# Attention softmax: where the division by the row sums is done, and which buffers the position products use

## The chip, the cores and the metric

The kernel runs on one core of one Trainium2 chip. A core has five engines with their own instruction streams: TensorE (PE in the profile, its weight loads are PEld), VectorE (DVE), ScalarE (ACT), GpSimd (POOL) and SyncE (SP), which here only issues transfers. Sixteen DMA engines move data between the memory on chip (SBUF) and DRAM. TensorE writes into a small accumulator memory (PSUM). The metric is the device time of one execution in microseconds (us); the median of three runs is given.

## The reference, cut to what matters

Two layers of attention over images, each with a group normalization ahead of it and a residual behind it. There are 4 images of 32 by 32 positions, so 1024 positions with 768 channels each, and 12 heads of 64 channels. All is in 32-bit floats. The second layer differs in the weights' layout, in biases on q, k and v, and in one more scale factor on q.

```python
qkv = x @ Wqkv                                   # x is normalized by groups first
q, k, v = ...                                    # (4 * 12, 1024, 64) each
rel_h = einsum('bhwc,hkc->bhwk', r_q, Rh)        # position terms: q times a table of
rel_w = einsum('bhwc,wkc->bhwk', r_q, Rw)        #   relative rows and columns
bias = rel_h[..., :, None] + rel_w[..., None, :]
scores = scale * einsum('bqc,bkc->bqk', q, k) + bias.reshape(B * hn, S, S)
attn = softmax(scores, axis=-1)                  # exp(scores - max) / sum
out = einsum('bqk,bkc->bqc', attn, v)            # the value product
return out @ Wproj + bproj                       # + residual outside
```

The division by the softmax's sum is a factor for each query row. It can be done on the 1024 probabilities of a row ahead of the value product, or on the 64 results of the row behind it.

## The kernel before

The work is cut into 8 images (2 layers of 4), in each 6 pairs of heads (called g, 48 in all), and in each pair 8 blocks of 128 queries (called n). A unit is one block of one pair: two heads, 128 queries, 1024 keys. Only TensorE's order is fixed by hand; on the other engines and on the transfer queue a scheduler at build time chooses the order. The three parts below are those that the change touches. SP issues nearly all transfers, in its own order, and an issue that has to wait holds those behind it.

```python
scpool = ctx.enter_context(tc.tile_pool(name="sc", bufs=6))   # 128 x 1024 score tiles
tbpool = ctx.enter_context(tc.tile_pool(name="tb", bufs=4))   # transposed, two blocks each
ptpool = ctx.enter_context(tc.tile_pool(name="pt", bufs=1))   # probabilities, keys on partitions
ps_s   = ctx.enter_context(tc.tile_pool(name="ps_s", bufs=3, space=PSUM))
ps_m   = ctx.enter_context(tc.tile_pool(name="ps_m", bufs=2, space=PSUM))

def project_in(g, which, i):          # q, k, v of pair g, half i: six matmuls "pj"
    if i == 0:
        pool, tag = (scpool, "sc") if which == 2 else (qkpool, "qk"[which])
        qkv_of[g, which] = pool.tile([P, S], FP, tag=tag, ...)    # v takes a score buffer
    ...                               # q leaves PSUM on ACT (L236, L238), k and v on DVE
    if which == 0:
        early.append(lambda: positions(g, i))
    ...

def positions(g, i):                  # position products "tp" (L276)
    ps = ps_s.tile([P, 2, 4, P], FP, tag="s", ...)
    ...                               # 8 small matmuls of q with the table
    t = scpool.tile([P, 4, 2, P], FP, tag="sc", name=f"t_{g}_{i}")   # a score buffer too
    nc.scalar.copy(t, ps.rearrange("p h j r -> p j h r"))         # L281
    nc.scalar.dma_start(out=td[i * HALF : (i + 1) * HALF, :]..., in_=t...)   # tdr<-t
    if i == 1:
        ...                           # 16 small reads from DRAM: rel<-tdr (L298), on SP

def biases(g, n):
    for h in range(2):
        sc = scpool.tile([P, HW, HW], FP, tag="sc", ...)
        nc.gpsimd.tensor_tensor(sc, <rel rows>, <rel columns>, ALU.add)      # L308

def scores(g, n):
    ps = [ps_s.tile([P, S], FP, tag="s", ...) for h in range(2)]
    ...                               # four matmuls "s" (L320)
    st = small.tile([P, 3, 2], FP, tag="sm", ...)
    for h in range(2):
        nc.vector.tensor_tensor_reduce(out=sc, in0=ps[h], in1=sc, ...,
                                       accum_out=st[:, 0, h : h + 1])        # L327: add, row max
        nc.scalar.activation(sc, sc, AF.Exp, bias=..., accum_out=st[:, 1, h : h + 1])   # L331
    nc.vector.reciprocal(st[:, 2, :], st[:, 1, :])                           # L335
    for h in range(2):
        nc.gpsimd.tensor_scalar(sc, sc, st[:, 2, h : h + 1], 1.0, ALU.mult, ALU.mult)   # L338

def turn(g, n):                       # keys onto partitions, by way of DRAM
    for h in range(2):
        nc.vector.transpose(tb[:, :, j, :], sc_of[g, n, h])                  # L356
        if j == 1:                    # every second block
            nc.sync.dma_start(out=td, in_=tb...)                             # L359: td<-tb
            nc.sync.dma_start(out=pt[:, quarter]..., in_=td...)              # L360: pt<-td

def weigh(g, half):                   # value products "av" of four blocks (L372)
    ...                               # 16 matmuls of 128 x 512, two heads side by side
    for q in range(2):
        nc.vector.tensor_copy(attn_of[g]..., av...)                          # L379
```

The main loop, cut. `todo` holds the projections of the next pair (36 matmuls) and parts of the output projection (12 matmuls "o", whose sums leave PSUM at L432 and L434); a block takes six of them.

```python
for at, (g, n) in enumerate(units):
    ...
    run(early)                        # position products and issues that have become possible
    scores(next unit)
    biases(unit after it)
    turn(g, n)
    take(todo, -(-left(todo) // (NT - n)))
    if n % 4 == 1 and at > 4:
        weigh(*(units[at - 2][0], n // 4 ^ 1))     # the half that ended two blocks ago
    run(ready)                        # v turned on TensorE, "vt" (L261)
```

Of the kernel before, what the change touches and what calls it, by code (L numbers as in the profile page):

```python
# [31 lines left out]
P = 128  # L32
# [16 lines left out]
def attention_blocks(ctx: ExitStack, tc: tile.TileContext, a: dict, out: bass.AP):  # L49
# [8 lines left out]
    qkpool = ctx.enter_context(tc.tile_pool(name="qk", bufs=2))  # L58
    vpool = ctx.enter_context(tc.tile_pool(name="v", bufs=2))
    scpool = ctx.enter_context(tc.tile_pool(name="sc", bufs=6))  # L60
    tbpool = ctx.enter_context(tc.tile_pool(name="tb", bufs=4))
    ptpool = ctx.enter_context(tc.tile_pool(name="pt", bufs=1))
    relpool = ctx.enter_context(tc.tile_pool(name="rel", bufs=2))
    iopool = ctx.enter_context(tc.tile_pool(name="io", bufs=4))
# [146 lines left out]
    def project_in(g, which, i):  # L211

        im, pair = divmod(g, NP)
        l = images[im][0]
        xn, w = xn_of[im], w_of[g, which]
        cols = slice(i * HALF, (i + 1) * HALF)
        if i == 0:
            pool, tag = (scpool, "sc") if which == 2 else (qkpool, "qk"[which])
            qkv_of[g, which] = pool.tile([P, S], FP, tag=tag, name=f"{'qkv'[which]}_{g}")
        to = qkv_of[g, which][:, cols]  # L220
        if which == 2:
            to = qkv_of[g, 2].rearrange("p (k j y) -> p y k j", y=4, k=NT)[:, 2 * i : 2 * i + 2]
        t = ps_m.tile([P, HALF], FP, tag="m", name=f"pj_{g}_{which}_{i}")
        for c in range(NC):
            nc.tensor.matmul(  # L225
                t, lhsT=w[:, c, :], rhs=xn[c][:, cols],
                start=(c == 0), stop=(c == NC - 1),
            )
            if c < NC - 1:
                yield True  # L230
        if which == 2:
            t = t.rearrange("p (y k j) -> p y k j", y=2, k=NT)
        bias = bqkv[:, which, pair : pair + 1]
        if which == 0:
            if l == 0:
                nc.scalar.activation(to, t, AF.Copy, scale=SCALE)  # L236
            else:
                nc.scalar.activation(to, t, AF.Identity, bias=bias, scale=SCALE * SCALE)  # L238
        elif l == 0:
            nc.vector.tensor_copy(to, t)  # L240
        else:
            nc.vector.tensor_scalar(to, t, bias, None, ALU.add)
        if which == 0:
            early.append(lambda: positions(g, i))
        if which == 2 and i == 1:
            late.extend([lambda: turn_values(g, 0), lambda: turn_values(g, 1)])
        if i == 1 and g + 1 < NPAIR:
            early.append(lambda: load_w(g + 1, which))
        if which == 2 and i == 1 and pair == NP - 1 and im + 1 < NI:
            early.extend([lambda: load_x(im + 1), lambda: norm_stats(im + 1)])  # L250
        yield True
# [12 lines left out]
    def positions(g, i):  # L264

        l = images[g // NP][0]
        q = qkv_of[g, 0]
        if i == 0:
            t_of[g] = dram2.tile([S, 2 * P], FP, tag="tdr", name=f"tdr_{g}")
            rel_of[g] = relpool.tile([P, 2, 2, NT, HW], FP, tag="rel", name=f"rel_{g}")  # L270
        ps = ps_s.tile([P, 2, 4, P], FP, tag="s", name=f"tp_{g}_{i}")
        for j in range(4):
            for h in range(2):
                rows = slice(h * D, (h + 1) * D)
                at = 4 * i + j
                nc.tensor.matmul(  # L276
                    ps[:, h, j, :], lhsT=q[rows, at * P : (at + 1) * P], rhs=tabs[l][rows, :],
                    start=True, stop=True,
                )
        t = scpool.tile([P, 4, 2, P], FP, tag="sc", name=f"t_{g}_{i}")  # L280
        nc.scalar.copy(t, ps.rearrange("p h j r -> p j h r"))  # L281
        td = t_of[g]
        nc.scalar.dma_start(
            out=td[i * HALF : (i + 1) * HALF, :].rearrange("(j p) r -> p j r", p=P),
            in_=t.rearrange("p j h r -> p j (h r)"),
        )
        if i == 1:
            for h in range(2):
                for ax in range(2):
                    for y in range(4):  # L290


                        at = HW * y * 2 * P + h * P + HW - 1 + 2 * HW * ax - (y if ax == 0 else 0)
                        src = bass.AP(
                            td.tensor, td.offset + at,
                            [[2 * P - ax, HW], [P * 2 * P - (4 if ax == 0 else 0), NT], [1, HW]],
                        )
                        nc.sync.dma_start(out=rel_of[g][32 * y : 32 * y + 32, h, ax, :, :], in_=src)  # L298


    sc_of, tb_of, pt_of, attn_of = {}, {}, {}, {}

    def biases(g, n):
        rel = rel_of[g]
# [8 lines left out]
    def scores(g, n):  # L313
        q, k = qkv_of[g, 0], qkv_of[g, 1]
        ps = [ps_s.tile([P, S], FP, tag="s", name=f"s_{g}_{n}_{h}") for h in range(2)]
        for i in range(2):
            cols = slice(i * HALF, (i + 1) * HALF)
            for h in range(2):
                rows = slice(h * D, (h + 1) * D)
                nc.tensor.matmul(  # L320
                    ps[h][:, cols], lhsT=q[rows, n * P : (n + 1) * P], rhs=k[rows, cols],
                    start=True, stop=True,
                )
        st = small.tile([P, 3, 2], FP, tag="sm", name=f"sm_{g}_{n}")
        for h in range(2):
            sc = sc_of[g, n, h].rearrange("p y x -> p (y x)")
            nc.vector.tensor_tensor_reduce(  # L327
                out=sc, in0=ps[h], in1=sc, scale=-1.0, scalar=BIG, op0=ALU.add, op1=ALU.min,
                accum_out=st[:, 0, h : h + 1],
            )  # L330
            nc.scalar.activation(  # L331
                sc, sc, AF.Exp, bias=st[:, 0, h : h + 1], scale=-1.0,
                accum_out=st[:, 1, h : h + 1],
            )
        nc.vector.reciprocal(st[:, 2, :], st[:, 1, :])  # L335
        for h in range(2):
            sc = sc_of[g, n, h].rearrange("p y x -> p (y x)")
            nc.gpsimd.tensor_scalar(sc, sc, st[:, 2, h : h + 1], 1.0, ALU.mult, ALU.mult)  # L338

    def turn(g, n):  # L340

# [23 lines left out]
    def weigh(g, half):  # L365
        if half == 0:
            attn_of[g] = apool.tile([P, S], FP, tag="attn", name=f"attn_{g}")
        av = ps_m.tile([P, HALF], FP, tag="m", name=f"av_{g}_{half}")
        for k in range(NT):
            for h in range(2):  # L370
                rows = slice(h * D, (h + 1) * D)
                nc.tensor.matmul(  # L372
                    av[rows, :], lhsT=v_of[g][:, k, rows],
                    rhs=pt_of[g, half, h][:, :, :, k, :].rearrange("p q r t -> p (q r) t"),
                    start=(k == 0), stop=(k == NT - 1),
                )
        for q in range(2):
            at = half * HALF + q * 2 * P
            nc.vector.tensor_copy(  # L379
                attn_of[g][:, at : at + 2 * P].rearrange("p (n r i) -> p r n i", n=2, r=4),  # L380
                av[:, q * 2 * P : (q + 1) * 2 * P].rearrange("p (r n i) -> p r n i", n=2, r=4),
            )


# [54 lines left out]

    early, late = [], []

    def run(todo):
        while todo:
            todo.pop(0)()
# [30 lines left out]
    with tc.manual_schedule(engines={mybir.EngineType.PE}):  # L477
# [13 lines left out]
        for at, (g, n) in enumerate(units):  # L491
            im, pair = divmod(g, NP)
            end = im + 1 == NI
            if n == 0:
                ins = prepare(g + 1) if g + 1 < NPAIR else []
                if pair < 3:
                    todo = ins + (put_out(im - 1, 1, range(4 * pair, 4 * pair + 4)) if im else [])
                elif pair < NP - 1:
                    todo = ins + ([] if end else put_out(im, 0, range(4 * pair - 12, 4 * pair - 8)))
                elif not end:  # L500
                    outs = put_out(im, 0, range(8, 12))
                    stages = [(staged(f), 0) for f in norm_apply(im + 1)]
                    todo = [x for both in zip(outs, stages) for x in both] + ins
            if end and pair == NP - 1 and n == 2:
                todo = put_out(im, 0, range(12))
            run(early)
            if at + 1 < len(units):
                scores(*units[at + 1])
            if at + 2 < len(units):
                biases(*units[at + 2])  # L510
            ready = late[:1]
            del late[:1]
            turn(g, n)
            take(todo, -(-left(todo) // (NT - n)))
            if n % 4 == 1 and at > 4:
                weigh(*(units[at - 2][0], n // 4 ^ 1))
            run(ready)
# [53 lines left out]
```

## Time and profile before

The three runs took 4016.77, 4021.23 and 4022.7 us; the median is 4021.23 us. One execution was profiled; its span is 4008.2 us.

| engine | busy, share of the span | largest group of instructions |
| --- | --- | --- |
| TensorE | 95% | L225, projections of q, k and v, 3456 records |
| VectorE | 58% | L356 transposes and L327 add with row maximum, 768 each |
| GpSimd | 57% | L308 position biases, 768 |
| ScalarE | 29% | L331 exponentials, 768 |
| 16 DMA engines | between 70% and 80% in most of the run | td<-tb and pt<-td, 384 transfers of 1 MB each |

A busy share is time in which at least one instruction of an engine runs. A matmul on 32-bit floats shows as two records. The profile's page also lists groups of instructions with what they waited for, the transfers with the time from issue to landing, and the waits by pairs of waiter and releaser; in a timeline the number in brackets is the idle time of the engine ahead of an instruction and what ended it. Names are those of the program's tiles: `sc` a score tile, `s` its PSUM source, `sm` the row maxima and sums, `tb`, `td` and `pt` the transposed probabilities on chip, in DRAM and back on chip, `tp`, `t`, `tdr` and `rel` the position terms on their way.

### The profile page before, as it was taken

Reading aid. Unit: us, or ns where it says so; the run is one execution under the profiler, and the core shown is the slowest. Engines: PE = TensorE matmul, PEld = TensorE weight load, DVE = VectorE, ACT = ScalarE, POOL = GpSimd, SP = SyncE. Lnnn points to the kernel's source line nnn. Section 1 sums busy time; section 2 is a strip of 40 time slices with the busy share of each in tenths; the row PEclk is TensorE's granted clock in tenths of the full one; section 3 lists DMA queues with packets and bytes.
Section 4 is the critical chain, followed back from the end, with each engine's and each line's share of the span. In section 5 each row is a group of like instructions: output and inputs, shape, how many; then the busy total and the mean of one; then the engine's idle time right before and its main releaser. Section 6 shows DMA issues by size and latency. Waiting matters only on the chain.

```text
span 4008.2 us, 39298 instructions
## 1 busy us (share of the span) xinstructions
PE 3795.4 (95%) x13056; PEld 1577.2 (39%) x13056; DVE 2324.9 (58%) x3520; ACT 1150.5 (29%) x1848; POOL 2300.8 (57%) x1555
## 2 busy tenths in 40 slices
PE   7989899999999999999999998999999999999998
PEld 3334333433344334444344343433344343434332
DVE  4555655547565565656665566555665566546653
ACT  2233223322232222322232223323233222322320
POOL 4656556655666546656556565655556565556661
PEclk9999999999999999999999999999999999999998
DMA  4777777878787787877877787878877788778867
GB/s 166 247 260 266 284 257 278 299 248 290 257 288 276 260 300 253 295 268 278 285 275 277 266 298 280 278 251 288 301 264 265 266 287 305 261 248 283 288 250 244
DMA packets 615612, 1084.89 MB, mean 271 GB/s; under 512 B 234481, under 2 KB 295153, under 8 KB 566257
## 3 DMA queue, kind: packets, MB, share of 16 engines
q1 hardware_dynamic: 564720, 1032.05, 73.6%
q10 hardware_dynamic: 50688, 50.34, 3.7%
q8 instruction: 103, 1.69, 0.2%
q14 instruction: 101, 0.82, 0.1%
HBM read 578.92 MB, written 503.32 MB: 270 GB/s over the span
## 4 chain that ended last, share of the span: by engine, by line
PE 61%; DMA 11%; DVE 10%; POOL 6%; ACT 5%; issue 5%; SPq 1%; ACTq 0%; DVEq 0%; POOLq 0%
PE pj L225 20%; PE av L372 17%; PE s L320 11%; PE o L425 9%; DMA tdr<-t 8%; DVE tb L356 4%; ACT sc L331 4%; POOL sc L308 3%; POOL sc L338 3%; DVE sc L327 3%; PE tp L276 3%; DMA pt<-td 2%; DVE st L155 1%; ACT t L281 1%; PE vt L261 1%
## 5 line engine op out<-in xcount | busy, mean ns | idle before, releaser
L308 POOL TENSOR_TENSOR sc<-rel 128x1024 f32<-128x1024 f32 x768 | 1451.6, 1910 | 578.2 <-DMA tdr<-t 341.4
L225 PE MATMUL pj<-xn,w 128*128 128x512 f32 x3456 | 1581.4, 607 | 1.1 <-DVE xn L201 1.1
L331 ACT ACTIVATE sc<-sc,sm 128x1024 f32<-128x1024 f32 x768 | 878.6, 1145 | 2063.0 <-DVE sm L327 1558.6
L338 POOL TENSOR_SCALAR sc<-sc,sm 128x1024 f32<-128x1024 f32 x768 | 849.1, 1118 | 1063.1 <-DVE sm L335 1028.8
L356 DVE STREAM_TRANSPOSE tb<-sc 128x1024 f32<-128x1024 f32 x768 | 917.9, 1226 | 741.5 <-POOL sc L338 740.3
L225 PEld LDWEIGHTS pj<-xn,w 128*128 128x128 f32 x3456 | 640.3, 192 | 924.5 <-issue 908.9
L327 DVE CUSTOM_DVE_ANT_0 sc<-s,sc 128x1024 f32<-128x1024 f32 x768 | 905.8, 1214 | 159.3 <-PE s L320 155.8
L320 PE MATMUL s<-k,q 64*128 64x512 f32 x3072 | 844.7, 623 | 54.3 <-DVE sm L327 54.3
L372 PE MATMUL av<-pt,v 128*64 128x512 f32 x3072 | 706.9, 606 | 34.1 <-DMA pt<-td 10.2
L425 PE MATMUL o<-attn,wo 128*128 128x512 f32 x1152 | 537.6, 615 | 26.3 <-DVE res L432 21.2
L320 PEld LDWEIGHTS s<-k,q 64*128 64x128 f32 x3072 | 294.0, 189 | 461.0 <-issue 288.7
L372 PEld LDWEIGHTS av<-pt,v 128*64 128x64 f32 x3072 | 264.4, 139 | 462.6 <-issue 369.1
L425 PEld LDWEIGHTS o<-attn,wo 128*128 128x128 f32 x1152 | 213.2, 193 | 333.8 <-issue 272.2
L335 DVE RECIPROCAL sm<-sm 128x2 f32<-128x2 f32 x384 | 63.5, 165 | 441.5 <-ACT sc L331 441.5
L379 DVE COPY attn<-av 128x256 f32<-128x256 f32 x192 | 71.9, 416 | 251.1 <-PE av L372 251.0
L281 ACT COPY t<-tp 128x1024 f32<-128x1024 f32 x96 | 97.1, 1012 | 285.4 <-PE tp L276 277.9
L276 PE MATMUL tp<-tab,q 64*128 64x128 f32 x1536 | 111.6, 285 | 42.3 <-ACT q L238 20.9
L331 ACT ACTIVATION_READ_ACCUMULATOR sc<-sc,sm 128x1 f32 x768 | 143.2, 186 | 0.0
L276 PEld LDWEIGHTS tp<-tab,q 64*128 64x128 f32 x1536 | 93.3, 187 | 108.9 <-ACT q L236 40.5
L262 ACT COPY v<-vt 128x512 f32<-128x512 f32 x96 | 55.9, 583 | 219.4 <-PE vt L261 218.4
L261 PE MATMUL vt<-ident,v 128*128 128x128 f32 x384 | 60.0, 280 | 34.1 <-DVE res L432 28.8
L261 PEld LDWEIGHTS vt<-ident,v 128*128 128x128 f32 x384 | 46.1, 142 | 92.5 <-DVE res L432 40.4
(45 smaller groups left out, 655.7 us busy)
## 6 DMA issues: line engine op xcount, KB each, us to landing
td<-tb SPq DMA_DIRECT2D x384, 1024.0 KB, 6.1
pt<-td SPq DMA_DIRECT2D x384, 1024.0 KB, 7.2
w<-in_wqkv SPq DMA_DIRECT2D x144, 384.0 KB, 7.2
tdr<-t ACTq DMA_DIRECT2D x96, 512.0 KB, 7.6
rel<-tdr SPq DMA_DIRECT2D x768, 32.0 KB, 2.0
part<-res SPq DMA_DIRECT2D x96, 256.0 KB, 5.3
res<-part SPq DMA_DIRECT2D x96, 256.0 KB, 5.1
wo<-in_wo SPq DMA_DIRECT2D x84, 192.0 KB, 4.4
```

What stands on the lines that cost most here:

```text
L225: nc.tensor.matmul(t, lhsT=w[:, c, :], rhs=xn[c][:, cols], start=(c == 0), stop=(c == NC - 1),)
L261: nc.tensor.transpose(t[:, j, :], qkv_of[g, 2][:, at * P : (at + 1) * P], ident)
L276: nc.tensor.matmul(ps[:, h, j, :], lhsT=q[rows, at * P : (at + 1) * P], rhs=tabs[l][rows, :], start=True, stop=True,)
L281: nc.scalar.copy(t, ps.rearrange("p h j r -> p j h r"))
L308: nc.gpsimd.tensor_tensor(sc, rel[:, h, 0, n, :].unsqueeze(2).to_broadcast([P, HW, HW]), rel[:, h, 1, n, :].unsqueeze(1).to_broadcast([P, ...
L320: nc.tensor.matmul(ps[h][:, cols], lhsT=q[rows, n * P : (n + 1) * P], rhs=k[rows, cols], start=True, stop=True,)
L327: nc.vector.tensor_tensor_reduce(out=sc, in0=ps[h], in1=sc, scale=-1.0, scalar=BIG, op0=ALU.add, op1=ALU.min, accum_out=st[:, 0, h : h + 1],)
L331: nc.scalar.activation(sc, sc, AF.Exp, bias=st[:, 0, h : h + 1], scale=-1.0, accum_out=st[:, 1, h : h + 1],)
L338: nc.gpsimd.tensor_scalar(sc, sc, st[:, 2, h : h + 1], 1.0, ALU.mult, ALU.mult)
L356: nc.vector.transpose(tb[:, :, j, :], sc_of[g, n, h])
L372: nc.tensor.matmul(av[rows, :], lhsT=v_of[g][:, k, rows], rhs=pt_of[g, half, h][:, :, :, k, :].rearrange("p q r t -> p (q r) t"), start=(k ...
L425: nc.tensor.matmul(t, lhsT=w[:, c - c0, :], rhs=attn_of[im * NP + c][:, cols], start=(c == c0), stop=(c == c1 - 1),)
```

## The change

The change does three things.

1. The probabilities stay undivided. The 1024-wide multiplication of every score tile on GpSimd (L338) goes. Row sums of four blocks are gathered in one tile, one reciprocal takes all eight columns, and a round trip over DRAM lays the 512 reciprocals of a head along the free dimension and repeats them over the head's 64 partitions (`rd`, `rb`). The value product is multiplied by them as it leaves PSUM. The wait of the transposes for GpSimd is meant to go.
2. The position copies `t` and the value projections `v` get two buffers of their own (`tmp`), so that they no longer take score buffers. One of four `tb` buffers is given up for the space.
3. In all pairs but the first of an image the position products come a block later, so that TensorE need not wait for q to leave PSUM.

```diff
-    tbpool = ctx.enter_context(tc.tile_pool(name="tb", bufs=4))
+    tbpool = ctx.enter_context(tc.tile_pool(name="tb", bufs=3))
+    tmppool = ctx.enter_context(tc.tile_pool(name="tmp", bufs=2))
+    rbpool = ctx.enter_context(tc.tile_pool(name="rb", bufs=2))
@@ project_in
-            pool, tag = (scpool, "sc") if which == 2 else (qkpool, "qk"[which])
+            pool, tag = (tmppool, "tmp") if which == 2 else (qkpool, "qk"[which])
@@
-            early.append(lambda: positions(g, i))
+            (later if pair else early).append(lambda: positions(g, i))
@@ positions
-        t = scpool.tile([P, 4, 2, P], FP, tag="sc", name=f"t_{g}_{i}")
+        t = tmppool.tile([P, 4, 2, P], FP, tag="tmp", name=f"t_{g}_{i}")
@@ scores
-        st = small.tile([P, 3, 2], FP, tag="sm", name=f"sm_{g}_{n}")
+        if n % 4 == 0:
+            st_of[g, n // 4] = small.tile([P, 3, 2, 4], FP, tag="sm", name=f"sm_{g}_{n}")
+        st, j = st_of[g, n // 4], n % 4
... the two accum_out and the bias now take column j of their head ...
-        nc.vector.reciprocal(st[:, 2, :], st[:, 1, :])
+    def spread(g, half):
+        st = st_of[g, half].rearrange("p a h n -> p a (h n)")
+        nc.vector.reciprocal(st[:, 2], st[:, 1])
+        rd = dram2.tile([2, HALF], FP, tag="rd", name=f"rd_{g}_{half}")
+        nc.sync.dma_start(out=rd.rearrange("h (n p) -> p (h n)", p=P), in_=st[:, 2])
+        rb = rbpool.tile([P, HALF], FP, tag="rb", name=f"rb_{g}_{half}")
+        rb_of[g, half] = rb
         for h in range(2):
-            sc = sc_of[g, n, h].rearrange("p y x -> p (y x)")
-            nc.gpsimd.tensor_scalar(sc, sc, st[:, 2, h : h + 1], 1.0, ALU.mult, ALU.mult)
+            nc.sync.dma_start(
+                out=rb[h * D : (h + 1) * D, :], in_=rd[h : h + 1, :].to_broadcast([D, HALF])
+            )
@@ weigh
-            nc.vector.tensor_copy(
-                attn_of[g][:, at : at + 2 * P].rearrange("p (n r i) -> p r n i", n=2, r=4),
-                av[:, q * 2 * P : (q + 1) * 2 * P].rearrange("p (r n i) -> p r n i", n=2, r=4),
+            nc.vector.tensor_tensor(
+                attn_of[g][...].rearrange("p (n r i) -> p n r i", n=2, r=4),
+                av[:, at : at + 2 * P].rearrange("p (r n i) -> p n r i", n=2, r=4),
+                rb_of[g, half][:, at : at + 2 * P].rearrange("p (n r i) -> p n r i", n=2, r=4),
+                ALU.mult,
             )
@@ main loop
             run(early)
+            early, later = later, early
@@
             turn(g, n)
+            if n % 4 == 3:
+                spread(g, n // 4)
```

The build of the changed kernel shows what the scheduler makes of this on the queue of SP. In 35 of the 48 pairs the 16 reads `rel<-tdr` of the next pair stood ahead of both `td<-tb` of blocks 2 and 3; now they stand between the two transfers that bring these blocks back, behind `pt<-td` of the first head and ahead of `pt<-td` of the second.

```
before:  REL x16 | td_3_0 td_3_1 pt_0<-td_3_0 pt_1<-td_3_1 | w_1 | td_5_0 td_5_1 ...
after:   td_3_0 td_3_1 pt_0<-td_3_0 | REL x16 | pt_1<-td_3_1 | rd w_1 td_5_0 rb rb td_5_1 ...
```

TensorE's order differs only in the place of the position products: before, those of q's second half came ahead of the scores of block 3, and now they come ahead of those of block 4.

More of the change, by code (lines that the diff above doesn't have):

```diff
@@ L298, in positions @@
                         nc.sync.dma_start(out=rel_of[g][32 * y : 32 * y + 32, h, ax, :, :], in_=src)
-    sc_of, tb_of, pt_of, attn_of = {}, {}, {}, {}
+    sc_of, st_of, tb_of, pt_of, rb_of, attn_of = {}, {}, {}, {}, {}, {}
     def biases(g, n):
@@ L328, in scores @@
                 out=sc, in0=ps[h], in1=sc, scale=-1.0, scalar=BIG, op0=ALU.add, op1=ALU.min,
-                accum_out=st[:, 0, h : h + 1],
+                accum_out=st[:, 0, h, j : j + 1],
             )
             nc.scalar.activation(
-                sc, sc, AF.Exp, bias=st[:, 0, h : h + 1], scale=-1.0,
-                accum_out=st[:, 1, h : h + 1],
-            )
-        nc.vector.reciprocal(st[:, 2, :], st[:, 1, :])
+                sc, sc, AF.Exp, bias=st[:, 0, h, j : j + 1], scale=-1.0,
+                accum_out=st[:, 1, h, j : j + 1],
+            )
+    def spread(g, half):
[5 more added lines that the diff above has]
+        rb_of[g, half] = rb
         for h in range(2):
-            sc = sc_of[g, n, h].rearrange("p y x -> p (y x)")
-            nc.gpsimd.tensor_scalar(sc, sc, st[:, 2, h : h + 1], 1.0, ALU.mult, ALU.mult)
+            nc.sync.dma_start(
+                out=rb[h * D : (h + 1) * D, :], in_=rd[h : h + 1, :].to_broadcast([D, HALF])
+            )
     def turn(g, n):
@@ L377, in weigh @@
         for q in range(2):
-            at = half * HALF + q * 2 * P
-            nc.vector.tensor_copy(
-                attn_of[g][:, at : at + 2 * P].rearrange("p (n r i) -> p r n i", n=2, r=4),
-                av[:, q * 2 * P : (q + 1) * 2 * P].rearrange("p (r n i) -> p r n i", n=2, r=4),
+            at = q * 2 * P
+            nc.vector.tensor_tensor(
+                attn_of[g][:, half * HALF + at : half * HALF + at + 2 * P].rearrange(
+                    "p (n r i) -> p n r i", n=2, r=4
+                ),
+                av[:, at : at + 2 * P].rearrange("p (r n i) -> p n r i", n=2, r=4),
+                rb_of[g, half][:, at : at + 2 * P].rearrange("p (n r i) -> p n r i", n=2, r=4),
+                ALU.mult,
             )
@@ L437, in project_out @@
         yield True
-    early, late = [], []
+    early, later, late = [], [], []
     def run(todo):
```

## The prediction

> **What bounds the kernel now.** I read the busy shares first, then the groups of instructions with their idle time, then the timeline of one ordinary pair of heads (the pair from 1588 to 1667 us). The page's first part and its rows for TensorE:
>
> ```profile
> PE 3795.4 (95%) x13056; PEld 1577.2 (39%) x13056; DVE 2324.9 (58%) x3520; ACT 1150.5 (29%) x1848; POOL 2300.8 (57%) x1555
> ...
> L320 PE MATMUL s<-k,q 64*128 64x512 f32 x3072 | 844.7, 623 | 54.3 <-DVE sm L327 54.3
> L372 PE MATMUL av<-pt,v 128*64 128x512 f32 x3072 | 706.9, 606 | 34.1 <-DMA pt<-td 10.2
> L425 PE MATMUL o<-attn,wo 128*128 128x512 f32 x1152 | 537.6, 615 | 26.3 <-DVE res L432 21.2
> ...
> L276 PE MATMUL tp<-tab,q 64*128 64x128 f32 x1536 | 111.6, 285 | 42.3 <-ACT q L238 20.9
> ...
> L261 PE MATMUL vt<-ident,v 128*128 128x128 f32 x384 | 60.0, 280 | 34.1 <-DVE res L432 28.8
> ```
>
> TensorE is busy 95% of the span, and nothing else is near that. Only its idle 213 us and what hides in the busy time can be won. The middle column is the idle time ahead of each kind of matmul: five rows make up 191 of the 213.
>
> The timeline shows more than these rows count. TensorE in that pair:
>
> ```profile
> 1633.57 1.16 PE L276 MATMUL tp<-tab,q 64*128 64x128 f32 x16
> 1634.56 1.89 PE L320 MATMUL s<-k,q 64*128 64x512 f32 x8
> 1636.38 5.42 PE L225 MATMUL pj<-xn,w 128*128 128x512 f32 x12
> 1641.73 1.99 PE L320 MATMUL s<-k,q 64*128 64x512 f32 x8
> 1643.64 5.42 PE L225 MATMUL pj<-xn,w 128*128 128x512 f32 x12
> 1648.99 1.12 PE L320 MATMUL s<-k,q 64*128 64x512 f32 x2
> 1651.31 1.98 PE L320 MATMUL s<-k,q 64*128 64x512 f32 x6 [1.20 <-DVE sm L327]
> 1653.22 5.42 PE L225 MATMUL pj<-xn,w 128*128 128x512 f32 x12
> 1658.57 2.75 PE L320 MATMUL s<-k,q 64*128 64x512 f32 x8
> 1661.25 5.42 PE L225 MATMUL pj<-xn,w 128*128 128x512 f32 x12
> 1666.59 5.87 PE L372 MATMUL av<-pt,v 128*64 128x512 f32 x26
> ```
>
> From start to start, undisturbed scores take 1.91 us (1641.73 to 1643.64) and a projection 5.35. At 1648.99 the scores took 4.23, at 1658.57 2.68: 3.1 us lost, of which only 1.20 is shown as idle. Why VectorE was late, from the timelines of GpSimd, VectorE and SP:
>
> ```profile
> 1644.13 1.91 POOL L308 TENSOR_TENSOR sc<-rel 128x1024 f32<-128x1024 f32 x1 [10.99 <-DMA tdr<-t]
> 1646.01 2.21 POOL L338 TENSOR_SCALAR sc<-sc,sm 128x1024 f32<-128x1024 f32 x2
> ```
> ```profile
> 1647.16 2.37 DVE L356 STREAM_TRANSPOSE tb<-sc 128x1024 f32<-128x1024 f32 x2 [6.77 <-POOL sc L338]
> ```
> ```profile
> 1644.06 7.73 SPq L298 DMA_DIRECT2D rel<-tdr  x16
> 1651.88 0.87 SPq L359 DMA_DIRECT2D td<-tb  x2
> 1656.12 2.94 SPq L360 DMA_DIRECT2D pt<-td  x2
> ```
>
> GpSimd sat 11 us for the landing of `tdr<-t`. This isn't data for the bias: the bias is to be written into a score buffer that the position copy `t` holds until its transfer ends. Behind it in GpSimd's queue stood the multiplication L338, behind that the transposes on VectorE (6.77 us), behind those the row maximum that frees the scores' PSUM, and so TensorE. The waits name it 46 times, once a pair, 341 us in total on GpSimd.
>
> **What the Trainium skill says.** "Perfetto Trace Analysis", Identifying the Most-Contended Engine: matmul busy time is no good measure because matmuls are pipelined. The trace agrees: a projection record has a mean of 607 ns, but 12 of them span 5.35 us from start to start, 446 ns each. So I count starts. "SBUF — State Buffer", Who interferes with whom: a VectorE instruction with at most one SBUF input, outside the two-port modes, doesn't contend with GpSimd. L327 reads PSUM and one SBUF tile, L356 one; L356 takes 1.25 and 1.20 us with GpSimd busy beside it or not. So I give nothing for faster VectorE instructions once L338 is gone. "DMA: Bandwidth & Descriptors", Rules for kernel authors: a last dimension that isn't contiguous becomes one descriptor per element, so a `rd` write should be 1024 pieces of 4 bytes. Same page, Anatomy of one DMA: a fixed cost of about 2 us per transfer, mostly the receipt of the write. The 32 KB reads `rel<-tdr` land in 2.0 us, which agrees; no run here shows 4-byte data yet.
>
> **The change part by part.**
>
> 1. Division moved. L338 goes: 768 x 1118 ns = 849 us of GpSimd, which then does 1452 us, 37%. None of it is on TensorE, but the transposes' wait for it (740 us on VectorE in the waits) goes, and so does the wait of the 384 reciprocals (441 us). They become 96, saving about 63.5 - 96 x 0.165 = 48 us of VectorE. The 192 copies of `av` (416 ns) become products of one PSUM and one SBUF tile; the residual add L434 of that kind takes 674 ns for twice the width, so I expect 0.35 to 0.45 us: no change. VectorE now runs row maximum, then transposes, with only the exponential (1.15 us) between.
>
> 2. Own buffers for `t` and `v`. The 341 us wait of GpSimd goes. With part 1 it removes the delay of VectorE twice over.
>
> 3. Position products a block later. The wait of L276 for q goes but in the first pair of each image (one in six): 42.3 x 5/6 = 35 us.
>
> Sum of the gain: an ordinary pair repeats every 78.7 us. From the starts its work is 8 scores x 1.91 + 6 projections x 5.35 + 2 value products x 7.1 + 12 output matmuls x 2 records x 0.43 + position products 2.0 + turning v 1.2 = 75.1, and about 0.3 for changes between kinds. So 3.3 us a pair are waste; x 48 = 158. The idle rows give the same order by another way: 54 (L320) + 35 (L276) + 29 (L261, VectorE late with `res`) + some 15 of L372 and 8 of L425 = 141, plus what is hidden as at 1658.57. I take 150. Some 17 us of pipeline start and about 20 us around the normalizations stay.
>
> 4. What it adds. In 35 pairs SP now issues the 16 `rel` reads ahead of the second head's `pt<-td`, which the value product of this half needs. In the pair above, position products ended at 1634.7, `tdr` landed and `rel` issue began at 1644.06, and ended at 1651.8: 17.1 us later. Then that `pt<-td` lands; the page's median is 7.2 us, and where before issued the second head's 5 us after the first's it took 6.2. That is 23.4 us behind the position products. TensorE, undisturbed, has three scores and three projections between: 3 x (1.91 + 5.35) = 21.8. So it would wait 1.6 us, x 35 = 56 us. This is the least certain term: with 1 us less in `tdr` it is 20, with 2 us more 125.
>
> 5. The round trip of reciprocals. 96 x 1024 = 98,304 packets of 4 bytes; the trace's 128-byte packets take 13 ns, so by that about 80 us over 16 engines, 2% of their span; the 12,288 packets of `rb`, 2 KB at 96 ns, add 74 us, another 2%. They are needed only when a value product ends, over 15 us after the reciprocal. I take 0 on the path, but the pieces may delay what is queued behind them.
>
> 6. `tb` from 4 to 3 buffers: the transposes of block 6's second head wait for `td_5_0`, which now stands behind the `rel` reads. I estimate that it lands some 24 us after the position products' end. The transpose could begin at about 21. This stall falls while TensorE is in the value product, ahead of block 7's scores: 0.
>
> Net: -150 + 56 = -94, so about 3925.
>
> **The rivals.** (a) SP is the new wait: the chain tdr, rel, pt ends later than TensorE's work in every ordinary pair, and takes all back. For it: before, the same chain with `td` in it ended just as `av` began (1656 + 2.94 + landing against 1666.59), so there was no slack. Against it: the `td` leg, 4.2 us of wait plus issue, is now ahead of `rel`. It would make 3960 to 4030. (b) 4-byte writes are far slower than their size: if a `rd` write takes 10 us or more, `rb` and the `td_5` behind it come late, the products wait in VectorE and hold PSUM. It would make 3970 to 4080. Nothing in this profile speaks for or against it. (c) TensorE is nearly all of the time anyway, so that only idle time goes and its busy time stays: 3895 to 3925 if `pt` is never late. Even without any waste, 158 us would be the most, so under 3860 I see nothing.
>
> **Range and chances.** The centre 3925 is 2.4% below 4021. The range 3875 to 3985 holds from (c) with all gained and no new wait to most of (a). The 2% line is at 3941; I put 0.62 below it, 0.34 within 2%, 0.04 above 4102, for (b) at its worst.
>
> **What would show it.** Right: no wait of GpSimd for `tdr<-t`; transposes waiting for L331's successor in name only, well under 200 us; L276 and L261 with under 10 us idle each; L320's wait for VectorE under 10; and a new wait of L372 for `pt<-td`, some 30 to 90 us, in the ordinary pairs. Wrong: L372's wait above 120 us (rival a), `rd` landing in over 8 us or L379's successor waiting for `rb` (rival b), or L320 still waiting for VectorE, which would say that I misread why it was late.

## The result, and the profile after

| | median of runs, us | range, us |
| --- | --- | --- |
| before | 4021.97 | 4016.77 to 4031.69 |
| after | 4372.61 | 4357.84 to 4376.86 |

The ratio is 1.086, with a 95% interval of 1.083 to 1.090: 8.6% slower. The profiled execution of the changed kernel spans 4375.2 us. From its page come the busy shares, the chain that ended last by engine, and the rows that answer to those shown of before:

```profile
PE 3885.3 (89%) x13056; PEld 1565.5 (36%) x13056; DVE 2308.5 (53%) x3232; ACT 1152.4 (26%) x1848; POOL 1461.8 (33%) x787
...
DMA 50%; PE 31%; SPq 7%; DVE 5%; issue 4%; ACT 2%; POOL 0%; DVEq 0%
...
L386 PE MATMUL av<-pt,v 128*64 128x512 f32 x3072 | 838.1, 660 | 247.4 <-DMA pt<-td 245.6
...
L322 PE MATMUL s<-k,q 64*128 64x512 f32 x3072 | 789.6, 622 | 52.6 <-DVE sm L332 52.6
...
L263 PE MATMUL vt<-ident,v 128*128 128x128 f32 x384 | 62.7, 288 | 77.2 <-DVE res L450 54.1
...
L278 PE MATMUL tp<-tab,q 64*128 64x128 f32 x1536 | 111.6, 285 | 11.9 <-ACT q L240 6.3
```

GpSimd fell from 57% to 33%, as meant, and the position products L278 hardly wait. But the value product L386 went from 34.1 us of idle time to 247.4, and its own records grew from 606 to 660 ns. The chain runs half of its time through transfers. The waits of the changed kernel name which ones (waiter, releaser, us in total, times, longest):

```profile
DVE tb L370 <- DMA td<-tb: 996.8, 126, 15.2
...
PE av L386 <- DMA pt<-td: 245.6, 61, 7.9
...
DVE tb L370 <- ACT sc L336: 55.9, 340, 0.4
```

The transposes waited for GpSimd before (740 us). That is gone, and 997 us for the landing of an older `td` stand in its place, 126 times, so 8 us each. SP's own waits, in the queue that issues these transfers, show a second new one:

```profile
SPq L374 <- DMA td<-tb: 956.4, 295, 9.9
SPq L350 <- DMA rd<-sm: 849.6, 90, 15.9
```

SP stands 850 us until the reciprocals have landed in DRAM. Half a pair of heads shows how it goes. SP's timeline of the changed kernel (start, duration, what is issued, how many):

```profile
1692.35 7.72 SPq L300 DMA_DIRECT2D rel<-tdr  x16
1700.11 1.28 SPq L374 DMA_DIRECT2D pt<-td  x1
1701.49 0.45 SPq L346 DMA_DIRECT2D rd<-sm  x1
1702.04 0.52 SPq L94 DMA_DIRECT2D w<-in_wqkv  x1
1702.66 0.49 SPq L373 DMA_DIRECT2D td<-tb  x1
1714.89 1.10 SPq L350 DMA_DIRECT2D rb<-rd  x2
1716.08 0.54 SPq L373 DMA_DIRECT2D td<-tb  x1
```

VectorE and TensorE in the same stretch; the bracket is the idle time ahead and what ended it:

```profile
1702.40 1.25 DVE L370 STREAM_TRANSPOSE tb<-sc 128x1024 f32<-128x1024 f32 x1 [0.16 <-ACT sc L336]
...
1718.72 1.25 DVE L370 STREAM_TRANSPOSE tb<-sc 128x1024 f32<-128x1024 f32 x1 [12.54 <-DMA td<-tb]
```
```profile
1704.99 1.07 PE L386 MATMUL av<-pt,v 128*64 128x512 f32 x2
1709.10 8.78 PE L386 MATMUL av<-pt,v 128*64 128x512 f32 x30 [3.04 <-DMA pt<-td]
```

`rd` carries 4 KB. It is issued at 1701.5, and only at 1714.9 can SP ask for `rb`, since it waits in its queue for `rd`. The `td` of 1702.66, 1 MB, lands at 1718.6, 16.0 us later, where 7.0 us is the median. So VectorE sits 12.5 us at its third `tb` buffer, and TensorE waits for a `pt` that was issued just ahead of `rd`. The windows of the changed kernel over this stretch (busy time of each engine, then TensorE's granted clock, the share of the DMA engines, GB/s):

```profile
1699.00:1705.00 6.00, 6.00 (x17) 2.21 (x13) 3.62 (x5) 2.39 (x4) 3.19 (x3) 1.00 0.58 165
1705.00:1709.10 4.10, 1.06 (x3) 0.18 (x3) 1.08 (x1) 0.00 (x0) 1.31 (x1) 1.00 1.81 171
1709.10:1713.00 3.90, 3.90 (x12) 1.32 (x14) 0.00 (x0) 0.00 (x0) 0.00 (x0) 0.60 0.41 38
1713.00:1717.80 4.80, 4.80 (x20) 1.28 (x16) 0.00 (x0) 0.00 (x0) 0.00 (x0) 0.97 0.85 188
```

Nearly all of the 1024 pieces of 4 bytes appear in the packet records between 1705 and 1707.3, at 9 ns each (median): there they look as cheap as the prediction had them. But from 1709.1 to 1713 the DMA engines move 38 GB/s (bytes of the packets that start there), with a 1 MB write outstanding, where the mean of the run is 254. The packets of other transfers show it directly: the twelve of 8 KB that start between 1707.1 and 1709.1 take 4.5 to 6.9 us each, where the median of that size is 0.31 us.

### The profile page after: what moved, and what is told of

Read it like the earlier page. It is cut to its first block, busy times and chain, and to the rows that moved or that the text cites. A ratio compares the mean times of both kernels' runs of the same rounds, so it can differ in the third digit from the quotient of the medians.

```text
span 4375.2 us, 38158 instructions
## 1 busy us (share of the span) xinstructions
PE 3885.3 (89%) x13056; PEld 1565.5 (36%) x13056; DVE 2308.5 (53%) x3232; ACT 1152.4 (26%) x1848; POOL 1461.8 (33%) x787
## 4 chain that ended last, share of the span: by engine, by line
DMA 50%; PE 31%; SPq 7%; DVE 5%; issue 4%; ACT 2%; POOL 0%; DVEq 0%
DMA td<-tb 17%; DMA pt<-td 13%; PE av L386 12%; PE pj L227 9%; DMA rd<-sm 7%; SPq L300 6%; PE s L322 5%; DMA tdr<-t 3%; PE o L443 2%; DVE tb L370 2%; PE tp L278 2%; ACT sc L336 2%; DMA mid<-res 2%; DMA wo<-in_wo 2%; DMA part<-res 2%
## 5 line engine op out<-in xcount | busy, mean ns | idle before, releaser
L370 DVE STREAM_TRANSPOSE tb<-sc 128x1024 f32<-128x1024 f32 x768 | 934.5, 1237 | 1053.5 <-DMA td<-tb 996.8
L386 PE MATMUL av<-pt,v 128*64 128x512 f32 x3072 | 838.1, 660 | 247.4 <-DMA pt<-td 245.6
L322 PE MATMUL s<-k,q 64*128 64x512 f32 x3072 | 789.6, 622 | 52.6 <-DVE sm L332 52.6
L443 PE MATMUL o<-attn,wo 128*128 128x512 f32 x1152 | 547.6, 621 | 71.2 <-DMA wo<-in_wo 26.9
L386 PEld LDWEIGHTS av<-pt,v 128*64 128x64 f32 x3072 | 269.9, 151 | 798.8 <-issue 641.2
L322 PEld LDWEIGHTS s<-k,q 64*128 64x128 f32 x3072 | 275.2, 190 | 417.5 <-issue 320.3
L393 DVE TENSOR_TENSOR attn<-av,rb 128x256 f32<-128x256 f32 x192 | 71.7, 414 | 215.4 <-PE av L386 163.4
L263 PE MATMUL vt<-ident,v 128*128 128x128 f32 x384 | 62.7, 288 | 77.2 <-DVE res L450 54.1
L278 PEld LDWEIGHTS tp<-tab,q 64*128 64x128 f32 x1536 | 93.2, 187 | 82.4 <-issue 54.2
L278 PE MATMUL tp<-tab,q 64*128 64x128 f32 x1536 | 111.6, 285 | 11.9 <-ACT q L240 6.3
L263 PEld LDWEIGHTS vt<-ident,v 128*128 128x128 f32 x384 | 46.1, 146 | 141.5 <-DVE res L450 70.9
L450 DVE SCALAR_TENSOR_TENSOR res<-o,bo,res 128x512 f32<-128x512 f32 x96 | 68.6, 721 | 49.8 <-PE o L443 33.8
L157 DVE BATCH_NORM_STATS2 st<-xn 128x6 f32<-128x512 f32 x96 | 59.7, 664 | 31.6 <-DMA xn<-in_x 18.2
```

What stands on the lines that cost most here:

```text
L263: nc.tensor.transpose(t[:, j, :], qkv_of[g, 2][:, at * P : (at + 1) * P], ident)
L278: nc.tensor.matmul(ps[:, h, j, :], lhsT=q[rows, at * P : (at + 1) * P], rhs=tabs[l][rows, :], start=True, stop=True,)
L322: nc.tensor.matmul(ps[h][:, cols], lhsT=q[rows, n * P : (n + 1) * P], rhs=k[rows, cols], start=True, stop=True,)
L386: nc.tensor.matmul(av[rows, :], lhsT=v_of[g][:, k, rows], rhs=pt_of[g, half, h][:, :, :, k, :].rearrange("p q r t -> p (q r) t"), start=(k ...
L443: nc.tensor.matmul(t, lhsT=w[:, c - c0, :], rhs=attn_of[im * NP + c][:, cols], start=(c == c0), stop=(c == c1 - 1),)
```

## Experiments

All times are medians; each ratio is to the kernel before, timed beside it, with its 95% interval. Runs marked * leave out the division of the probabilities: the value products leave PSUM times a tile of ones.

| run | what it is | us | ratio | interval | rd lands, us |
| --- | --- | --- | --- | --- | --- |
| e1_no_trip * | after without the round trip | 3829.7 | 0.951 | 0.949 to 0.953 | none |
| e2_write_only * | after with the rd write alone | 4211.7 | 1.046 | 1.043 to 1.049 | 13.1 |
| e10_pitch8 * | e2, a 4-byte piece every 8 bytes | 4025.6 | 1.000 | 0.999 to 1.002 | 10.4 |
| e9_pitch64 * | e2, every 64 bytes | 3812.8 | 0.948 | 0.946 to 0.950 | 7.9 |
| e5_spaced * | e2, every 512 bytes | 3803.6 | 0.945 | 0.942 to 0.948 | 7.3 |
| e6_32bytes * | e2, 128 pieces of 32 bytes | 3804.2 | 0.945 | 0.942 to 0.949 | 7.0 |
| e3_rows | after, reciprocals turned on chip, written as rows | 3823.8 | 0.949 | 0.947 to 0.952 | not told |
| e7_part1 | before + division moved, by rows | 3976.7 | 0.988 | 0.985 to 0.991 | |
| e4_own_later | before + own buffers + later positions | 3999.9 | 0.993 | 0.991 to 0.995 | |
| e11_rows_early | e3 without later positions | 3953.8 | 0.983 | 0.982 to 0.985 | |
| e8_rows_tb4 | e3 with four tb, one rb buffer | 3850.9 | 0.957 | 0.954 to 0.959 | |
| e12_rows_defer | e3, rb asked for a block later | 3834.9 | 0.954 | 0.952 to 0.955 | |

My theory after the result was that the 4-byte write itself holds up the DMA engines, and that everything else in the change is a gain. The rival was that the order of SP's queue does it: `rel` behind `td`, or SP standing for `rd`.

**e1_no_trip.** The round trip goes, all else stays.

```diff
     def spread(g, half):
-        nc.vector.reciprocal(...); rd write; rb reads
+        rb_of[g, half] = rb_one          # a constant tile of ones
```

> The changed kernel without the round trip of the reciprocals: the value product is multiplied by a constant tile of ones, so the division is left out (the product instruction stays). Theory A (the round trip is the cause): 3900 to 3960 us, the wait of the transposes for td<-tb falls from 997 us to under 150, the value product's wait for pt<-td from 246 to 20-90. Rival B (the new order of the rel reads and the third tb buffer are the cause, the trip only adds): over 4150 us, both waits over half of what they are.

3829.7 us: without the trip the change is 4.9% faster than before, 70 us under what was expected of theory A. The whole loss of 543 us (4372.6 - 3829.7) is the trip's, and none of it is the new place of the `rel` reads: in the same 35 pairs they stand between the two `pt` here too, and the value product waits little:

```profile
L378 PE MATMUL av<-pt,v 128*64 128x512 f32 x3072 | 722.5, 598 | 26.4 <-DMA pt<-td 26.2
```

**e2_write_only.** The write stays, and nobody reads it.

```diff
         nc.sync.dma_start(out=rd.rearrange("h (n p) -> p (h n)", p=P), in_=st[:, 2])
-        rb = rbpool.tile(...); two reads rb<-rd
+        rb_of[g, half] = rb_one
```

> As the run without the trip, but the scattered write rd<-sm stays (1024 pieces of 4 bytes, 96 times); nothing reads it and nothing waits for it except the reuse of its buffer. Division left out. Theory A1 (the write clogs the 16 DMA engines for all that is behind it): 4150 to 4370 us, rd still lands in over 10 us and td/pt behind it in over 10. Theory A2 (the write is slow but alone; the harm is SP standing 850 us in wait for it ahead of td_5_1): within 1% of the run without the trip.

4211.7 us. With nothing waiting for it, the write alone costs 382 us over e1, 4.0 us for each of 96. The remaining 161 us to the changed kernel are the rest of the trip: SP standing for `rd`, the `rb` reads and who waits for them. So both theories hold a part, and the write has the larger one.

**e3_rows.** The reciprocals are turned on VectorE first, so that DRAM gets 32 rows of 128 bytes.

```diff
-        nc.vector.reciprocal(st[:, 2], st[:, 1])
-        nc.sync.dma_start(out=rd.rearrange("h (n p) -> p (h n)", p=P), in_=st[:, 2])
+        nc.gpsimd.memset(rs, 1.0)                       # rs, rt: 128 x 32
+        nc.vector.reciprocal(rs[:, 0:8], st[:, 1])
+        nc.vector.transpose(rt, rs)
+        for b in range(4):
+            nc.sync.dma_start(out=rd[:, 32*b : 32*b+32], in_=rt[32*b : 32*b+8, :])   # rd: 8 x 128
```

> The changed kernel, complete, with the reciprocals turned on VectorE by one 32x32-block transpose (128x32) first, so that the write is 4 transfers of 8 rows of 128 bytes in place of 1024 pieces of 4 bytes; the spreading reads stay. Theory A: rd lands in 2 to 3 us, SP's wait for it falls from 850 us to under 250, time within 40 us of the run without the trip, so 3900 to 3990. Rival B: over 4150.

3823.8 us, all of the computation in it: a ratio to before of 0.949 (0.947 to 0.952), and 549 us under the changed kernel. From its page:

```profile
PE 3697.5 (97%) x13056; PEld 1528.2 (40%) x13056; DVE 2333.5 (61%) x3328; ACT 1151.3 (30%) x1848; POOL 1466.6 (38%) x883
...
L322 PE MATMUL s<-k,q 64*128 64x512 f32 x3072 | 778.9, 620 | 11.6 <-DVE sm L332 11.6
L391 PE MATMUL av<-pt,v 128*64 128x512 f32 x3072 | 700.6, 596 | 7.2 <-DMA pt<-td 4.7
```

The time is 76 us under the range expected. The value product waits 7.2 us in all, the scores 11.6. The 96 added turns cost VectorE 212 ns each. SP's wait for the reciprocals is 216 us instead of 850:

```profile
SPq L355 <- DMA rd<-rt: 216.4, 103, 6.9
```

**e5_spaced, e6_32bytes, e9_pitch64, e10_pitch8.** Each is e2 with another place for the pieces. They tell the number of pieces from where they lie.

```diff
-        rd = dram2.tile([2, HALF], ...)                 # e2: 4-byte pieces, neighbours from 128 partitions
-        nc.sync.dma_start(out=rd.rearrange("h (n p) -> p (h n)", p=P), in_=st[:, 2])
+        rd = dram2.tile([P, 8, P], ...)                 # e5; [P, 8, 16] in e9, [P, 8, 2] in e10
+        nc.sync.dma_start(out=rd[:, :, 0], in_=st[:, 2])
+        rd = dram2.tile([P, 8], ...); nc.sync.dma_start(out=rd, in_=st[:, 2])        # e6
```

> As the write-only run (division left out, nothing reads rd), still 1024 pieces of 4 bytes a write, but every piece goes to a block of 512 bytes of its own in DRAM. Theory C (pieces of different DMA engines that fall into the same few blocks of DRAM hold each other up): rd lands in under 5 us and the time is within 60 us of the run without the trip (3830). Theory N (it's the number of tiny pieces, wherever they go): rd lands in over 10 us, 4100 to 4300 us.

> As the write-only run, the same 4 KB, but as 128 pieces of 32 bytes, one for each partition, side by side in DRAM (division left out, nothing reads it). Theory N: 128 pieces cost an eighth, rd lands in 2 to 4 us, 3830 to 3890 us. Theory C: still about 16 pieces to a block of 512 bytes in place of 128, so between, 4 to 8 us, 3850 to 4000.

> As the write-only run (division left out), 1024 pieces of 4 bytes, one every 64 bytes of DRAM, the 8 of one partition next to each other. If pieces collide only within 64 bytes: like the run with 512 bytes (3804 us). If a block of 512 bytes is what they collide in (8 pieces, all of one partition and so of one transfer share): 3850 to 4200 us if such pieces collide, else like 3804.

> As the run before in this list, but one piece every 8 bytes: a partition's 8 pieces share 64 bytes, and 8 partitions share 512. The same number of pieces, the smallest distance that keeps the same order. If neighbours within 64 bytes hold each other up even when they come from one partition: rd lands in over 10 us, 4000 to 4220. If only pieces of different partitions in the same block do: between 3804 and 4000.

The same 1024 pieces of 4 bytes cost nothing that can be seen when they lie 512 bytes apart (3803.6) or 64 (3812.8), 222 us over e5 when they lie 8 bytes apart, and 408 when they touch. So neither the number of pieces nor their size is enough to cost anything. For 1024 pieces of 4 bytes it is how close in DRAM they land. The 128 pieces of 32 bytes in e6 touch as well and are free, so closeness alone isn't enough either. The row of the value product follows, e10 first, then e5:

```profile
L383 PE MATMUL av<-pt,v 128*64 128x512 f32 x3072 | 780.0, 621 | 116.0 <-DMA pt<-td 114.0
```
```profile
L383 PE MATMUL av<-pt,v 128*64 128x512 f32 x3072 | 710.7, 595 | 13.4 <-DMA pt<-td 12.4
```

The packet records say what the close pieces do to the rest. Packets that took over 3 us: 677 in the changed kernel (519 of them of 8 KB), 559 in e2, 94 in e10, and none in before, e3, e5, e6 and e9. The expectation that a spaced write would land in under 5 us failed: it takes 7.3, about what `td` (7.4) and `pt` (6.8) take in that run. In e6 the landing, 7.0, is in theory C's range, and the time is under both theories' ranges. One thing isn't separated. In e10 the pieces within 64 bytes come from one partition and eight partitions share 512 bytes, while in the changed kernel neighbouring pieces come from different partitions. What happens inside the DMA engines or the memory no trace here shows.

**e7_part1, e4_own_later, e11_rows_early.** Parts of the change alone, with the harmless write.

```diff
 e7: before, with e3's spread and product (sc shared, four tb, positions early)
 e4: before, +tmp pool of two, tb 4 -> 3, +(later if pair else early); L339 stays on GpSimd
 e11, against e3:
-            (later if pair else early).append(lambda: positions(g, i))
+            early.append(lambda: positions(g, i))
```

> The kernel before with the division moved alone (its write as rows of 128 bytes): position copies and v still take score buffers, four tb buffers, position products early. If the division on GpSimd was what held the transposes, most of the gain of the complete kernel with rows (3824) is here: 3840 to 3900. If the shared score buffers were (as I predicted: GpSimd's 341 us wait for tdr<-t), the wait stays but no longer delays the transposes of earlier blocks, and the time is 3900 to 3980.

> The kernel before with own buffers for the position copies and v (tb 3) and the position products a block later; the division stays on GpSimd ahead of the transposes. If what I read of the kernel before is right, GpSimd's 341 us wait for tdr<-t goes and L276's wait with it: 3890 to 3960 us. If the later place of the rel reads (ahead of both pt<-td of blocks 2 and 3) delays the value product: 3960 to 4060, with L372 waiting over 80 us for pt<-td. If the third tb buffer is short: transposes wait over 200 us for td<-tb.

> The complete kernel with rows (3824 us), but the position products early, as before. This is the worth of part 3 alone, and of the place of the rel reads. By step 3 of the prediction TensorE's wait for q comes back: 30 to 40 us more, 3855 to 3865. By step 4 the second head's pt<-td is no longer behind the rel reads: up to 56 us less. So 3800 to 3865; L278's idle time over 35 us, L391's wait for pt under 5.

Alone, the moved division brings 1.2%, own buffers with later positions 0.7%, and moved division with own buffers 1.7%. All three together (e3) bring 5.1%. The waits suggest why. In e7 GpSimd's wait for the position copy's landing does not go but doubles (341 us before), and the value product is late:

```profile
POOL sc L309 <- DMA tdr<-t: 654.0, 77, 15.9
PE av L390 <- DMA pt<-td: 97.9, 43, 7.0
```

In e4 that wait of GpSimd is gone, but in 35 pairs the 16 `rel` reads stand ahead of both `pt` in SP's queue, and the value product waits as in e7:

```profile
PE av L373 <- DMA pt<-td: 99.3, 40, 7.8
```

e11 was expected at 3800 to 3865 us and took 3953.8. The timeline of one pair points to SP's queue; TensorE's follows, then SP's wait over the whole run (150.8 us in e3):

```profile
2100.10 7.75 SPq L300 DMA_DIRECT2D rel<-tdr  x16
2107.95 1.52 SPq L378 DMA_DIRECT2D td<-tb  x2
2112.38 2.79 SPq L379 DMA_DIRECT2D pt<-td  x2
```
```profile
2119.70 1.07 PE L391 MATMUL av<-pt,v 128*64 128x512 f32 x2
2121.86 7.08 PE L391 MATMUL av<-pt,v 128*64 128x512 f32 x30 [1.08 <-DMA pt<-td]
```
```profile
SPq L300 <- DMA tdr<-t: 364.7, 49, 10.6
```

SP waits for `tdr`, spends 7.75 us on 16 reads for the next pair, and only then sends `td`, which the value product 12 us on needs back. In e3 the position products come a block later, and their reads fall behind `td`:

```profile
2104.50 1.47 SPq L378 DMA_DIRECT2D td<-tb  x2
2110.27 0.37 SPq L379 DMA_DIRECT2D pt<-td  x1
2114.55 7.82 SPq L300 DMA_DIRECT2D rel<-tdr  x16
2122.42 0.45 SPq L379 DMA_DIRECT2D pt<-td  x1
```
```profile
2128.51 7.52 PE L391 MATMUL av<-pt,v 128*64 128x512 f32 x32
```

There is no gap in the 32 value products, though their second `pt` was asked for only 6.1 us ahead.

A count of TensorE from start to start shows in one table where the time goes. From each record's start to the next one's, the undisturbed distance of its kind is taken off (429 ns for 512 columns of a projection, 214 ns for a score or value product), and the sum is set against the same sum of e3, in us:

| lost against e3 | before | e7 | e4 | e11 | after |
| --- | --- | --- | --- | --- | --- |
| between scores | 106 | -22 | 0 | -22 | 50 |
| at and in value products | 36 | 150 | 192 | 138 | 379 |
| ahead of position products | 33 | 25 | 0 | 25 | 0 |
| all places, with those not listed | 187 | 152 | 177 | 127 | 552 |
| difference of the profiled spans | 187 | 152 | 177 | 128 | 554 |

The last two rows must agree, as distances from start to start add up to the span: the table says where time is lost, not why. Against before, e7, e4 and e11 win 106 to 128 us between the scores and lose 102 to 156 at the value products.

**e8_rows_tb4.** Four `tb` buffers again; for the space, one `rb` buffer instead of two.

```diff
-    tbpool = ...bufs=3      rbpool = ...bufs=2
+    tbpool = ...bufs=4      rbpool = ...bufs=1
```

> The complete kernel with rows, but four tb buffers and one rb buffer. The transposes' wait for td<-tb (357 us with three) should fall below 60. If that wait lay beside TensorE's work, as step 6 of the prediction took it, the time stays within 10 us of 3824; if not, up to 40 us less. A single rb buffer could hold the spreading read until the product of the half before: L398's wait for rb would show it.

3850.9 us, 27 more than e3, where 10 were allowed for. The transposes no longer wait for `td`, which cost VectorE 357 us in e3, yet the time doesn't fall, as it should if that wait lies beside TensorE's work when `rd` is quick. It isn't shown cleanly: by starts, the scores come out 22 us better than in e3 and the value products 44 worse. No product waits for `rb`, and whether the single `rb` buffer costs the time wasn't tried.

**e12_rows_defer.** The two `rb` reads are asked for a block after the write, which was meant to spare SP the wait.

```diff
             if n % 4 == 3:
                 spread(g, n // 4)              # writes rd
+            if n % 4 == 0 and at:
+                spread_back(previous half)     # reads rb
```

> The complete kernel with rows, but the spreading reads are asked for a block later, so that SP stands less in wait for rd (216 us with rows). In the second half of a pair the read now stands after the output's transfers. If SP's wait costs time: 3800 to 3815 us. If it lies beside other work: within 8 us of 3824.

3834.9 us, 11 more than e3. But the wait that the edit was to lessen is still there, 216 us as in e3:

```profile
SPq L361 <- DMA rd<-rt: 216.0, 97, 7.4
```

In 57 of the 96 halves of pairs the scheduler left the reads behind the same issues as in e3 (in 39 of them `w` and one `td`); in 36 they moved behind the output's transfers. So the run shows another order of the queue, and what SP's wait costs stays open. e3 remains the best complete version.

## Why the prediction was wrong

- **Step 5, the round trip: this is the step that failed.** It took the packets' own time, 98,304 at 13 ns, for the whole cost and wrote "0 on the path". The packets' own time was near enough (9 ns). The cost was what they did to others: 382 us by the write alone (e2 against e1; 408 against e5), and 161 more by the rest of the trip, of which SP's stand for the landing (850 us) is the likely part, as e3 has the `rb` reads too and is no slower than e1. "The pieces may delay what is queued behind them" was the right sentence, with no number given to it. The Trainium skill's "DMA: Bandwidth & Descriptors", Rules for kernel authors, was rightly read as one descriptor per element, but e5 has just as many elements and is free. The same page's Specifications say that below 512 bytes the engine reads, modifies and writes; that does not order the runs either, as 4 bytes at a pitch of 64 were free. The fixed cost of about 2 us in the same page's Anatomy of one DMA, which the prediction took for any transfer, is given there for transfers issued by GpSimd; on SP's queue here the harmless writes landed in 7.0 to 7.9 us.
- **Rival (b)** named the sign: `rd` over 8 us (13.9 measured). Its size was too small, 3970 to 4080. It named a late `td_5`, but put the damage on products that wait for `rb`, and the waits give those 28 us. VectorE's wait at its three `tb` buffers for `td` (997 us) and the value product's for `pt` (246 us) were far larger. A chance of 0.04 for slower was too little for a kind of transfer of which no trace had a single example.
- **Steps 1 and 2** held. GpSimd does 1462 us (1452 predicted), the reciprocals fell from 63.5 to 15.5 us (48 predicted), the product takes 414 ns (350 to 450 predicted), and GpSimd's wait for `tdr` is gone. Transposes wait 56 us for the exponential (under 200 predicted). One product in step 1 is off: 768 x 1118 ns is 859 us, and 849 is the page's busy time, where overlaps count once.
- **The sum of the gain was too small.** It was 150, and no more than 158; e3 shows 187 by profiled spans, 201 by medians. The floor of a pair was right: 75.4 us predicted, 75.2 the median of e3. What was off was the period before, 78.7 us of one pair; the median of 47 periods (between the first value products of neighbouring pairs) is 79.1, and (79.1 - 75.2) x 48 = 187. By rows, the idle time between scores fell by 43 us from before to e3 (54.3 to 11.6), and 106 us were won there. "Under 3860 I see nothing" was wrong by 36 us.
- **Step 3** took 35 us for the idle time ahead of the position products. That idle time fell by 30. But the step is worth 130 us (e11 against e3), and the table has 138 us at the value products; that the order of SP's queue is behind it is read from its timeline.
- **Step 4 had the wrong sign.** It booked 56 us for a late second `pt`. In e3 all of this waiting is 5 us. The chain was estimated at 23.4 us behind the position products; in e3's pair they end at 2106.98 and the value products run from 2128.51 without a gap, so it took at most 21.5. More important, the step looked only at the `pt` that the reads now hold up and not at the two `td` that they no longer do, which by e11 is worth more.
- **Step 6** isn't contradicted by e8, where `rd` is quick, but isn't shown cleanly either. With the slow `rd` of the changed kernel its premise broke: the `td` shown landed after 16.0 us, not in time.
- **Signs.** The sign set for rival (a), more than 120 us of the value product's wait for `pt`, came up too, at 246 us; its cause was (b), as e1 has the same place of the `rel` reads and waits 26 us. L278 fell to 11.9 and L322 to 52.6 us; with a harmless write L322 is at 11.6. L263 was to fall under 10 and rose to 77, and is 50 in e3: a wait for VectorE's residual work that I had ascribed to the transposes' delay, and whose cause stays open.

## What to carry to other kernels

A small write to DRAM is judged by what lies next to what: where pieces of 4 bytes touch or lie 8 bytes apart, turn the tile on chip first, give each piece 64 bytes of its own, or write 32 bytes at a time. All three writes were free here; only the first was run with the reads behind it. For a kind of transfer that the trace doesn't hold, measure its effect on the others before giving it zero. When several waits end at the same join, one part alone can hand most of its gain to the next, so parts are to be tried together as well as apart, with the order of the issuing queue written out.

## What the runs showed of the hardware

- Ninety-six writes of 1024 touching 4-byte pieces cost 382 us; with 8 bytes from piece to piece 196 (e10 against e1), with 64 or 512 nothing. During one, the transfers fell to 38 GB/s for 4 us after nearly all of the pieces' own packets had ended, and 8 KB packets of another transfer took up to 6.9 us instead of 0.31.
- Idle time on TensorE came with a second cost. In the window from 1709.1 to 1713 us, right after a gap of 3 us, the granted clock was 0.60, and the 30 value products took 8.78 us where 32 took 7.52 in e3. After e11's gap of 1.08 us nothing of the kind is seen: 30 took 7.08. Over the whole run the granted clock was 0.95, against 0.99 in e3, and 247 us of idle time at the value products stand for 379 lost. In the changed kernel the granted clock fell to half during, or within 2 us of, 56 of the 59 gaps of TensorE over 3 us, but only 2 of the 99 between 0.5 and 2 us. Its value products were busy at half clock for 183 us (3 in e3), by which some 90 us of the 379 are the clock's, an estimate from these figures.
- Some differences of 10 to 26 us were not explained: e5 and e6, with a write that nobody reads, are 26 us faster than e1 without it, and e12, whose queue has another order, is 11 us slower than e3.
